# Coupling rows in column tiles and spread through DRAM, a room reserve that falls with attention's open buffers, and maxima added last in the score banks

## Chip, core and metric

The kernel runs on one core of one Trainium2 chip. The metric is device time in microseconds of that core, from the first to the last instruction and what lies around them; lower is better. The engines of the core are named as in the profile: PE (TensorE, matrix products; PEld is its weight load), DVE (VectorE), ACT (ScalarE), POOL (GpSimd) and SP (SyncE, which here issues every transfer).

## What is computed

Input `x` is 8 batches of 1024 tokens of 512 values, and `ctx` is 8 batches of 64 rows of 512 values; everything is float32.

- Attention: `x = x + Wo·attn(LN(x), ctx)` with 16 heads of 32 values. Queries and keys are rotated by one fixed phase per head, and each token attends to the 64 context rows of its batch.
- Feed-forward: with `out = LN(x)`, three cycles of `out = out + c·twist(out)` run. `twist` permutes and negates the four quarters of the 512 values. `c` is one number for each token and cycle: a network 512 → 512 → 256 → 128 → 1 with gelu after each hidden layer and a sigmoid at the end, times 0.3, plus a number per batch from a second small network of the mean over tokens, scaled by `adaptive_range`. At the end `x = x + out`.

## The kernel before, in words

**Work and its pieces.** The 8192 tokens are cut into 16 halves of 512 (`halves`, two for each batch). Attention runs over all halves first; then the feed-forward runs over "parts". `PARTS` cuts the first 14 halves into one part of 512 tokens each and the last two halves into two parts of 256 each, which makes 18 parts. `part_from_last[0]` counts them from 18 down to 1. Between the two phases `x` and the normalised `x` lie in DRAM (`x2d`, `xnd`).

**Numbers.** Most products are made of three matmuls in the type fp32r (`mm3`, lines 407 to 412): every operand is split into a high and a low half. A few products are plain float32 matmuls.

**Attention of a half** (`attn_half`, line 712). `qp` makes the queries, `sp` the approximate scores of which DVE takes the maximum per head, `mp` turns the maxima so that they lie along rows (`mT`), and the group of lines 772 to 785 builds four score banks `sT`: four matmuls of `hsel` with `mT` write minus the maximum into each whole bank (`start=True`), and then eight matmuls of `kT` with `qf` add the scores on 64 of the 128 partitions each. ACT takes the exponential into `pT`. `dn` sums the exponentials by 16 matmuls for each of two `k`, in column tiles: each writes only 32 of 128 partitions. The reciprocals go to DRAM (`rd`), and come back spread over partitions (`rb`, lines 810 to 820); `ap` and `op` make the output.

**Feed-forward of a part** (`ffn_part`, line 1017, W = 512 or 256 tokens). Stage A and B make the products `K`, `A` and `B`, which hold the first layer before any coupling: the input of cycle 1 is `A + c0·B`, and of cycle 2 it is `(1 - c0·c1)·A + (c0 + c1)·B`. `rest(cyc, h1)` (line 1048) makes the other layers: banks `l2`, `l3` (both `mm3`) and `l4`. In cycles 0 and 1, `l4` is one plain float32 matmul of `w4b` (the last layer's one column repeated 128 times) with `f3` over all W columns, so that the coupling row appears on all 128 partitions; in cycle 2 there are W/128 matmuls with `f3` as weights and one column. Line 1101 takes the tanh on ACT and line 1102 the scaling on DVE; the result `c` has 128 x W values in cycles 0 and 1. Lines 1121 to 1125 make `al = 1 - c0·c1` and `be = c0 + c1` over 128 x W. For the end of the part (`fin`) the first row of each goes to DRAM as `row` and comes back as `cc`, one value per token and partition (lines 1140 to 1146); POOL makes small factors from it, and ACT and DVE combine them with `x2` and `xt` into `out`. With `late`, an operation of cycle 2's start, the loads of `x2` and `xt` (2 MB for a part of 512) are held back.

**What orders the work.** Nothing is issued as it is written. `Plan` (line 119) notes every operation or group with its engine, its reads and writes and a cost in microseconds, and `schedule` (line 218) then walks an imagined clock: whenever an engine is free, it takes the ready operation with the lowest priority number whose buffers fit. A priority is the place in the text plus shifts by stage (`SHIFT`) and by part (`LAST`, and `TAIL` after time `FINALE`). Buffers live in `r4` (38 rooms of 4 KB per partition), `r2` (16 of 2 KB) and 8 PSUM banks; `CAPS` limits how many one kind may hold. The order so found is issued as it stands, so on the chip each engine keeps to it and waits where an operand is late.

**The reserve.** While any operation of attention is not done (`early_left`), an operation of the feed-forward may take a room of `r4` only if `KEEP` = 13 stay free (lines 205 to 206):

```
        for room, bs in need.items():
            keep = self.keep.get(room, 0) if op.late and self.early_left else 0
            if len(self.rooms[room]) < len(bs) + keep:
                return False
```

The functions the change touches, and what calls them:

Of the kernel before, what the change touches and what calls it, by code (L numbers as in the profile page):

```python
# [26 lines left out]
EPS = 1e-5  # L27
ROOMS4, ROOMS2 = 38, 16
GATE = 12
KEEP = 13  # L30
WIDE = 4
POOLED = 99
PLAIN = [(1, 1), (1, 2)]
CAPS = {'xb': 8, 'wn': 5, 'bv': 1, 'bo': 1, 'jm': 1, 'rt': 1, 'kbd': 2, 'vbd': 2, 'pT': 9, 'acc': 2, 'w3': 3, 'w2f': 1, 'w3f': 1, 'h2': 9, 'w4': 1, 'gw2': 1, 'gw3': 1, 'fxn': 2, 'fs': 2, 'f1': 12, 'AB': 14, 'f2': 11, 'f3': 2, 'c': 10, 'x2': 4, 'xe': 13, 'aT': 5, 'wg': 6, 'w2': 2, 'h1': 5, 'xna': 14, 'xnf': 6, 'xT': 6, 'fxT': 10, 'p': 6, 'sp': 4, 'pp': 2, 'ap': 4, 'op': 2, 'qp': 3, 'xp': 1, 'K': 4, 'A': 4, 'B': 7, 'l2': 5, 'l3': 4, 'l4': 5, 'ct': 3, 'qf': 5, 'qr': 3, 'rb': 4, 'mT': 2, 'mw': 1, 'sT': 8, 'mp': 3, 'dn': 1}
PARTS = [1, 1, 1, 1, 1, 1, 1, 1, 1, 1, 1, 1, 1, 1, 2, 2]
LAST = {4: -100, 2: -280, 1: -300}
FINALE = 1180
TAIL = {('fin', 4): 360, ('c1', 6): -57, ('load', 3): -330, ('A', 3): -389, ('B', 3): -170, ('c0', 3): -360, ('c1', 3): -130, ('c2', 3): 88, ('fin', 3): -160, ('fin', 6): -215, ('c0', 1): -350, ('fin', 5): 375, ('fin', 1): -170, ('c0', 4): 20, ('load', 6): 53, ('A', 6): 106, ('B', 6): 198, ('c0', 6): 157, ('c2', 6): 61, ('B', 4): 107, ('c0', 2): 110, ('c2', 4): 52, ('c2', 5): 416, ('load', 1): -320, ('A', 1): -24, ('B', 1): 73, ('c1', 1): -40, ('c2', 1): 33, ('A', 2): -40, ('load', 4): -117, ('A', 5): 50, ('load', 5): -136, ('B', 5): 150, ('c0', 5): 93, ('c1', 5): -264, ('fin', 2): 400, ('load', 2): 81, ('c2', 2): 30, ('B', 2): 120, ('c1', 4): 110}
SHIFT = {'ln1': 61, 'q': 175, 'm': 184, 's': -75, 'o': -41, 'pp': -40, 'av': 32, 'ln2': -260, 'load': -303, 'A': -70, 'B': -16, 'c0': -85, 'c1': 8, 'c2': 120, 'fin': -68}


def ts(i, n):
    return slice(i * n, (i + 1) * n)
# [3 lines left out]
    return t.bitcast(F32)  # L47

# [15 lines left out]
class Buf:  # L64


    def __init__(self, make, shape, room=None, tag=None, cap=0):
        self.make, self.shape, self.room, self.tag, self.cap = make, shape, room, tag, cap
        self.ap = None
        self.writers, self.readers = {}, {}  # L70
        self.left = 0
        self.slot = None


class View:
# [47 lines left out]
class Plan:  # L123


    def __init__(self, tc):
        self.tc, self.nc, self.ops, self.items = tc, tc.nc, [], None
        self.rooms, self.pools, self.caps = {}, {}, {}
        self.gates, self.stage = [], (None, 0)

        self.late, self.early_left, self.keep = False, 0, {}
# [35 lines left out]
    def add(self, cost, items, also):  # L167
        op = Op()
        op.engine, op.cost, op.calls, op.n = items[0][0], cost, [i[2] for i in items], len(self.ops)
        op.deps, op.users, bufs = set(self.gates), [], {}  # L170
        for _, _, _, reads, writes, _ in items:
            for v in reads:
                for k in v.grains():
                    if k in v.buf.writers:
                        op.deps.add(v.buf.writers[k])
                    v.buf.readers.setdefault(k, set()).add(op)
                bufs[id(v.buf)] = v.buf
            for v in writes:
# [8 lines left out]
        op.deps.discard(op)  # L187
        op.marks = [m for i in items for m in i[5] if isinstance(m, AF)]
# [24 lines left out]

    def schedule(self):
# [9 lines left out]
        now, seq = 0.0, itertools.count()  # L224
        while done < len(ops):
            for e in engines:
                if free[e] > now:
# [29 lines left out]
            while events and events[0][0] <= now + 1e-9:  # L257
# [1 line left out]
                if op is None:  # L259
                    continue  # L260
                done += 1
                self.early_left -= not op.late
                for b in op.bufs:
                    b.left -= 1
                    if b.left == 0:
# [19 lines left out]
class Engine:  # L285
# [3 lines left out]
    def __getattr__(self, method):  # L289
        def call(*args, **kw):  # L290
# [14 lines left out]
            def issue():  # L305
                f = getattr(getattr(self.plan.nc, self.name), method)
                f(*map(real, args), **{k: real(a) for k, a in kw.items()})  # L307

            self.plan.note(self.name, cost, issue, reads, outs, args)

        return call
# [37 lines left out]
def tile_xattn_ffn(  # L349
# [364 lines left out]
    def attn_half(b, h, xb, xnT):  # L714
# [53 lines left out]
        for k in range(2):  # L768
# [248 lines left out]
    def ffn_part(b, h, t0, n, xT):  # L1017
# [25 lines left out]
        for m in range(NC):  # L1043
            j, i = m // 2, m % 2
            p = product("B", m, 2)
            pl.vector.tensor_tensor(Bt[j][:, i, :], p, Bt[j][:, i, :], ALU.add)

        def rest(cyc, h1):
            nmc = f"{nm}_{cyc}"
            p = [bank([P, W], "l2", f"l2_{nmc}_{m}") for m in range(2)]  # L1050
# [33 lines left out]
                low(hL, f2[:, dc, :], hH)  # L1084
                mm3(p, w3p[0][:, dc, :], w3p[1][:, dc, :], hH, hL, dc == 0, dc == 1)
            gelu(f3, p, o3)
            if cyc < CYCLES - 1:
                p = bank([P, W], "l4", f"l4_{nmc}")
                c = t2([P, W], "c", f"c_{nmc}")
                pl.tensor.matmul(p, lhsT=w4b, rhs=f3, start=True, stop=True)  # L1090
            else:
# [3 lines left out]
                with pl.group(also=(c,)):  # L1095
                    for t in range(n):
# [4 lines left out]
            activation(c, p, AF.Tanh, bias=hb[:, 0:1], scale=0.5)  # L1101
            pl.vector.tensor_scalar(c, c, ar3, ca[:, b : b + 1], ALU.mult, ALU.add)
            return c

        def wide(t):
            return t.rearrange("p (o k) -> p o k", o=1).to_broadcast([P, 2, W])

        stage("c0")
        c0 = rest(0, h1)
        stage("c1")  # L1110
        h1, f1 = [], two(W, "f1", f"f1_{nm}_1_")
        for j in range(NC // 2):
# [5 lines left out]
            h1.append(f)  # L1118
        c1 = rest(1, h1)
        stage("c2")  # L1120
        al = t2([P, W], "c", f"al_{nm}")
        be = t2([P, W], "c", f"be_{nm}")
# [15 lines left out]
        stage("fin")  # L1138

        cc = small([P, 2, n], "cc", f"cc_{nm}", 2)  # L1140
        row = pl.fixed(dram.tile([1, 2, W], F32, name=f"row_{nm}"), [1, 2, W], F32)
        for k, t in enumerate((al, be)):
            with pl.group(cost=(0.1, 2.0)):
                pl.sync.dma_start(out=row[:, k, :], in_=t[:1, :])
# [19 lines left out]
        pl.gpsimd.tensor_scalar(rc[:, 4, :], pc[:, 3, :], -1.0, None, ALU.mult)  # L1164
        stage("c2")
        c2 = rest(2, h1)
        stage("fin")
        fa = small([P, 5, n], "fa", f"fa_{nm}", 2)
        wide_c = c2.rearrange("p (o t) -> p o t", o=1).to_broadcast([P, 5, n])
# [74 lines left out]
```

## Time and profile before

| | us |
|---|---|
| time, median of 3 runs (1316.57 to 1321.34) | 1318.05 |
| the profiled execution's own time | 1320.79 |
| span in its trace | 1319.0 |
| PE busy in the span | 1275.5 (97%) |
| DVE busy | 1110.2 (84%) |
| ACT busy | 859.7 (65%) |
| POOL busy | 346.6 (26%) |

The span runs from the first to the last instruction in the trace; the profiled execution's own time is 1.8 us longer. In the trace a line such as `L307 PE MATMUL l<-f,w4b 128*128 128x512` is an instruction of the line that issues everything (307), with its engine, the buffer it writes (without its number: `l` is `l2`, `l3` or `l4`), those it reads, the weights' shape (128*128: 128 rows by 128 columns; 128*32: a column tile) and its output's shape. A plain float32 matmul appears as two records, an fp32r one as one. The start of each record is measured; its length includes the way through the array, so the time a matmul takes from PE is read from the distance of starts.

### The profile page before, as it was taken

To read this page: it belongs to the slowest core of one execution; us is meant where nothing else is said; L and a number is where in the kernel's file an instruction comes from. 1 tells how busy PE (TensorE), PEld (TensorE's weight loads), DVE (VectorE), ACT (ScalarE), POOL (GpSimd) and SP (SyncE) were. 2 spreads that over 40 slices of the span, in tenths; PEclk is the share of its full clock that TensorE was granted. 3 is DMA by queue.
4 is the path that set the end of the run, shared out by engine and by line. 5 is a ranking of instruction groups with operands and counts; after the bars stand their busy time and mean duration, and the time that the engine had idled before them with its cause. 6 is when DMAs were issued, how large, how long until landed. Compare 5 with 4: busy or idle time off the path is not lost.

```text
span 1319.0 us, 21356 instructions
## 1 busy us (share of the span) xinstructions
PE 1275.5 (97%) x7907; PEld 994.9 (75%) x7907; DVE 1110.2 (84%) x1823; ACT 859.7 (65%) x1499; POOL 346.6 (26%) x426
## 2 busy tenths in 40 slices
PE   7999999999999999987999999999999999999996
PEld 6867776766767676755788888887888888888996
DVE  6767878787888787867869988899989999899997
ACT  3753545454553636433468878987889778888988
POOL 3501425152433424322201120112203121011271
PEclk9999999999999999998999999999999999999998
DMA  6313424243334444264302432324313233133224
GB/s 224 120 34 112 150 77 165 76 144 96 134 110 136 125 133 130 98 177 151 106 33 65 128 128 73 102 83 128 129 64 120 73 128 128 64 101 92 97 65 160
DMA packets 96152, 147.17 MB, mean 112 GB/s; under 512 B 25592, under 2 KB 47380, under 8 KB 96048
## 3 DMA queue, kind: packets, MB, share of 16 engines
q1 hardware_dynamic: 96048, 145.81, 34.6%
q8 instruction: 62, 1.02, 0.3%
q14 instruction: 42, 0.34, 0.1%
HBM read 93.80 MB, written 51.97 MB: 111 GB/s over the span
## 4 chain that ended last, share of the span: by engine, by line
PE 58%; DVE 6%; ACT 3%; issue 1%; DMA 1%; POOL 0%; SPq 0%; ACTq 0%; DVEq 0%
PE l L307 26%; PE op L307 6%; PE qp L307 3%; PE xp_f L307 2%; PE B_3p L307 2%; PE sT L307 2%; PE B_0p L307 2%; PE B_1p L307 2%; PE B_2p L307 2%; PE K_2p L307 2%; PE K_3p L307 2%; PE K_0p L307 2%; PE K_1p L307 2%; PE A_1p L307 1%; PE A_2p L307 1%; PE A_3p L307 1%
## 5 line engine op out<-in xcount | busy, mean ns | idle before, releaser
L307 PE MATMUL l<-h,w2H 128*128 128x512 f32 (+1 forms) x832 | 246.5, 381 | 0.1
L307 PEld LDWEIGHTS l<-h,w2H 128*128 128x128 f32 x832 | 149.6, 189 | 30.5 <-issue 3.6
L307 POOL TENSOR_TENSOR pc<-cc,rs 128x4 f32<-128x4 f32 (+1 forms) x18 | 22.2, 1231 | 507.3 <-DMA cc<-row 398.7
L307 PE MATMUL l<-h,w2L 128*128 128x512 f32 (+1 forms) x416 | 154.2, 371 | 0.0
L307 ACT ACTIVATE f<-l,bcol 128x512 f32<-128x512 f32 (+1 forms) x162 | 99.8, 635 | 28.5 <-PE l L307 26.9
L307 DVE TENSOR_TENSOR h<-f,h 128x1024 fp32r<-128x1024 f32 x84 | 102.1, 1218 | 12.9 <-ACT h L307 10.7
L307 ACT ACTIVATE f<-f,bcol 128x512 f32<-128x512 f32 x112 | 76.3, 721 | 46.0 <-DVE f L307 45.9
L307 POOL TENSOR_TENSOR acc<-acc,xnf 128x512 f32<-128x512 f32 x64 | 88.8, 1388 | 28.6 <-ACT xnf L307 25.2
L307 POOL TENSOR_TENSOR xb<-xb,bo_b 128x512 f32<-128x512 f32 x64 | 81.7, 1303 | 49.4 <-ACT xna L307 45.1
L307 DVE TENSOR_REDUCE mx<-sp 128x8 f32<-128x512 f32 x128 | 83.5, 680 | 9.9 <-PE sp L307 9.6
L307 ACT ACTIVATE pT<-sT 128x512 f32<-128x512 f32 x128 | 66.3, 612 | 36.7 <-PE sT L307 21.3
L307 PEld LDWEIGHTS l<-h,w2L 128*128 128x128 f32 x416 | 78.4, 188 | 13.7
L307 ACT CAST h<-f 128x1024 fp32r<-128x1024 f32 x84 | 88.0, 1053 | 0.7
L307 ACT CAST xT_a_0H<-xp_a 128x512 fp32r<-128x512 f32 x32 | 18.8, 587 | 97.7 <-PE xp_a L307 97.7
L307 ACT ACTIVATE xna<-xb,mb_a,rs_a 128x512 f32<-128x512 f32 x64 | 47.6, 829 | 51.2 <-DVE mb_a L307 38.9
L307 DVE TENSOR_TENSOR xb<-op,xb 128x512 f32<-128x512 f32 x64 | 44.2, 690 | 40.5 <-PE op L307 40.3
L307 POOL TENSOR_TENSOR rs<-rs,mhalf 128x4 f32<-128x4 f32 x16 | 19.4, 1215 | 205.7 <-DVE rs L307 205.1
L307 DVE TENSOR_SCALAR pT<-pT 128x1024 f32<-128x1024 f32 x64 | 44.5, 695 | 30.1 <-ACT pT L307 29.5
L307 DVE TENSOR_TENSOR f<-f,A 128x1024 f32<-128x1024 f32 x56 | 67.7, 1214 | 0.0
L307 ACT ACTIVATE x<-x,fa 128x256 f32<-128x256 f32 x128 | 65.3, 592 | 2.6 <-DVE fa L307 2.6
L307 ACT ACTIVATE xnf<-xb,mb,rs 128x512 f32<-128x512 f32 x64 | 47.4, 807 | 23.1 <-DVE mb L307 19.2
L307 DVE SCALAR_TENSOR_TENSOR x<-xt,fa,x 128x256 f32<-128x256 f32 x128 | 55.6, 480 | 6.2 <-ACT x L307 6.1
(399 smaller groups left out, 3737.3 us busy)
## 6 DMA issues: line engine op xcount, KB each, us to landing
xb<-in_x_dram SPq DMA_DIRECT2D x32, 512.0 KB
rb<-rd SPq DMA_DIRECT2D x128, 128.0 KB
x2d<-xb SPq DMA_DIRECT2D x32, 512.0 KB
xnd<-xnf SPq DMA_DIRECT2D x64, 256.0 KB
fxn<-xnd SPq DMA_DIRECT2D x32, 512.0 KB
x<-x2d SPq DMA_DIRECT2D x32, 512.0 KB
xt<-x2d SPq DMA_DIRECT2D x64, 256.0 KB
out_dram<-x SPq DMA_DIRECT2D x32, 512.0 KB
```

Source lines behind the costliest of these rows:

```text
L307: f(*map(real, args), **{k: real(a) for k, a in kw.items()})
```

## The change

- **Compact couplings.** Except for the last two parts (`DIRECT` = 2), `l4` becomes, in all three cycles, W/128 plain float32 matmuls with 32 columns of weights, each over 128 tokens and writing 32 partitions of one 128 x 128 bank. Tanh and scaling then run on 128 x 128 (64 x 128 in parts of 256), and so do `be` and `al`, whose last step moves from ACT to DVE. Each row is written to DRAM from one partition in 32 (`row_of`) and read back: `c0`, `be` and `al` over all 128 partitions x W (`spread`), and the cycle-2 row as one value per token and partition. `cc` is read by two transfers in place of one.
- **Reserve.** An operation of the feed-forward keeps free the smaller of 14 rooms and the number of attention's `r4` buffers that have not been given a room yet.
- **Scores.** The eight `kT` matmuls come first (`start=True` on 64 partitions each) and the four with the maxima last.
- **Planner.** It adds 0.18 or 0.1 us where PE changes to or from plain float32; caps are changed (among others `h2` 9 to 11, `f1` 12 to 14, `f2` 11 to 7, `c` 10 to 12, `x2` 4 to 6, `h1` 5 to 8, `xT` 6 to 9, `fxT` 10 to 12), and so are many shifts (`ln2` -260 to 165, `c2` 120 to 302, `c1` 8 to 115, `fin` -68 to 83) and the tail's entries; `FINALE` 1180 to 1160.

```diff
-KEEP = 13
+KEEP = 14
 WIDE = 4
+DIRECT = 2
...
+        op.keep = self.keep if self.late else {}
         op.late = self.late
-        self.early_left += not op.late
+        if not op.late:
+            for b in op.bufs:
+                if not b.counted:
+                    b.counted = True
+                    self.early_bufs[b.room] = self.early_bufs.get(b.room, 0) + 1
...
-            keep = self.keep.get(room, 0) if op.late and self.early_left else 0
+            keep = min(op.keep.get(room, 0), self.early_bufs.get(room, 0))
...
+                        if b.counted:
+                            self.early_bufs[b.room] -= 1
...
+                if e == "tensor" and not op.turn:
+
+                    busy += CHANGE[op.plain] if op.plain != plain else 0.0
+                    plain = op.plain
...
-                for g in range(4):
-                    q = slice(DK * g, DK * g + DK)
-                    pl.tensor.matmul(
-                        ps4[g], lhsT=hsel[q, ts(k, 2), :].rearrange("p r j -> p (r j)"),
-                        rhs=mT[q, :], start=True, stop=False,
-                    )
                 for r in range(2):
                     for g in range(4):
                         q = slice(DK * g, DK * g + DK)
                         pl.tensor.matmul(
                             ps4[g][ts(r, LC), :], lhsT=kT[q, 2 * k + r, ts(b, LC)],
-                            rhs=qf[k][q, r, :], start=False, stop=True,
+                            rhs=qf[k][q, r, :], start=True, stop=False,
                         )
+                for g in range(4):
+                    q = slice(DK * g, DK * g + DK)
+                    pl.tensor.matmul(
+                        ps4[g], lhsT=hsel[q, ts(k, 2), :].rearrange("p r j -> p (r j)"),
+                        rhs=mT[q, :], start=False, stop=True,
+                    )
...
+        compact = not 0 < part_from_last[0] <= DIRECT
...
-            if cyc < CYCLES - 1:
+            if compact:
+
+                p = bank([P, P], "l4", f"l4_{nmc}")
+                p = p[: DK * n, :]
+                c = small([P, P], "cs", f"c_{nmc}", 4)[: DK * n, :]
+                with pl.group(cost=0.27, also=(c,)):
+                    for t in range(n):
+                        pl.tensor.matmul(
+                            p[ts(t, DK), :], lhsT=w4b[:, :DK], rhs=f3[:, ts(t, P)],
+                            start=True, stop=True,
+                        )
+            elif cyc < CYCLES - 1:
...
+        def row_of(c, name):
+
+            r = pl.fixed(dram.tile([1, W], F32, name=f"{name}_{nm}"), [1, W], F32)
+            with pl.group(cost=(0.47, 2.0)):
+                if compact:
+                    pl.sync.dma_start(
+                        out=r.rearrange("o (t p) -> (o t) p", p=P), in_=c[0 : DK * n : DK, :]
+                    )
+                else:
+                    pl.sync.dma_start(out=r, in_=c[:1, :])
+            return r
+
+        def spread(r, name):
+            c = t2([P, W], "c", f"{name}_{nm}")
+            with pl.group(cost=(0.47, 2.5)):
+                pl.sync.dma_start(
+                    out=c,
+                    in_=r.via(lambda a: a.rearrange("o w -> (o w)").partition_broadcast(P)),
+                )
             return c
...
-        c0 = rest(0, h1)
+        c0 = c0s = rest(0, h1)
+        if compact:
+            c0 = spread(row_of(c0, "c0r"), "c0")
...
-        pl.vector.tensor_tensor(al, c0, c1, ALU.mult)
-        pl.scalar.activation(al, al, AF.Identity, bias=1.0, scale=-1.0)
-        pl.vector.tensor_tensor(be, c0, c1, ALU.add)
+        pl.vector.tensor_tensor(be, c0s, c1, ALU.add)
+        pl.vector.tensor_tensor(al, c0s, c1, ALU.mult)
+        pl.vector.tensor_scalar(al, al, -1.0, 1.0, ALU.mult, ALU.add)
+        be_r, al_r = row_of(be, "ber"), row_of(al, "alr")
+        if compact:
+            be, al = spread(be_r, "be"), spread(al_r, "al")
...
-        with pl.group(cost=(0.5, 4.0)):
-            pl.sync.dma_start(out=cc, in_=row.rearrange("o k (t p) -> p (o k) t", p=P))
+        for k, r in enumerate((al_r, be_r)):
+            with pl.group(cost=(0.5, 4.0)):
+                pl.sync.dma_start(out=cc[:, k, :], in_=r.rearrange("o (t p) -> p (o t)", p=P))
...
         c2 = rest(2, h1)
+        if compact:
+            c2_r, c2 = row_of(c2, "c2r"), small([P, n], "c2", f"c2_{nm}", 2)
+            with pl.group(cost=(0.5, 4.0)):
+                pl.sync.dma_start(out=c2, in_=c2_r.rearrange("o (t p) -> p (o t)", p=P))
```

More of the change, by code (lines that the diff above doesn't have):

```diff
@@ L29 @@
 GATE = 12
-KEEP = 13
+KEEP = 14
 WIDE = 4
+DIRECT = 2
 POOLED = 99
 PLAIN = [(1, 1), (1, 2)]
-CAPS = {'xb': 8, 'wn': 5, 'bv': 1, 'bo': 1, 'jm': 1, 'rt': 1, 'kbd': 2, 'vbd': 2, 'pT': 9, 'acc': 2, 'w3': 3, 'w2f': 1, 'w3f': 1, 'h2': 9, 'w4': 1, 'gw2': 1, 'gw3': 1, 'fxn': 2, 'fs': 2, 'f1': 12, 'AB': 14, 'f2': 11, 'f3': 2, 'c': 10, 'x2': 4, 'xe': 13, 'aT': 5, 'wg': 6, 'w2': 2, 'h1': 5, 'xna': 14, 'xnf': 6, 'xT': 6, 'fxT': 10, 'p': 6, 'sp': 4, 'pp': 2, 'ap': 4, 'op': 2, 'qp': 3, 'xp': 1, 'K': 4, 'A': 4, 'B': 7, 'l2': 5, 'l3': 4, 'l4': 5, 'ct': 3, 'qf': 5, 'qr': 3, 'rb': 4, 'mT': 2, 'mw': 1, 'sT': 8, 'mp': 3, 'dn': 1}
+CAPS = {'xb': 8, 'wn': 5, 'bv': 1, 'bo': 1, 'jm': 1, 'rt': 1, 'kbd': 2, 'vbd': 2, 'pT': 9, 'acc': 2, 'w3': 3, 'w2f': 1, 'w3f': 1, 'h2': 11, 'w4': 1, 'gw2': 1, 'gw3': 1, 'fxn': 2, 'fs': 4, 'f1': 14, 'AB': 14, 'f2': 7, 'f3': 4, 'c': 12, 'x2': 6, 'xe': 13, 'aT': 7, 'wg': 6, 'w2': 2, 'h1': 8, 'xna': 14, 'xnf': 8, 'xT': 9, 'fxT': 12, 'p': 6, 'sp': 4, 'pp': 2, 'ap': 4, 'op': 2, 'qp': 3, 'xp': 1, 'K': 4, 'A': 6, 'B': 5, 'l2': 6, 'l3': 6, 'l4': 3, 'ct': 3, 'qf': 4, 'qr': 5, 'rb': 4, 'mT': 2, 'mw': 1, 'sT': 8, 'mp': 4, 'dn': 1}
@@ L35 @@
 PARTS = [1, 1, 1, 1, 1, 1, 1, 1, 1, 1, 1, 1, 1, 1, 2, 2]
-LAST = {4: -100, 2: -280, 1: -300}
-FINALE = 1180
-TAIL = {('fin', 4): 360, ('c1', 6): -57, ('load', 3): -330, ('A', 3): -389, ('B', 3): -170, ('c0', 3): -360, ('c1', 3): -130, ('c2', 3): 88, ('fin', 3): -160, ('fin', 6): -215, ('c0', 1): -350, ('fin', 5): 375, ('fin', 1): -170, ('c0', 4): 20, ('load', 6): 53, ('A', 6): 106, ('B', 6): 198, ('c0', 6): 157, ('c2', 6): 61, ('B', 4): 107, ('c0', 2): 110, ('c2', 4): 52, ('c2', 5): 416, ('load', 1): -320, ('A', 1): -24, ('B', 1): 73, ('c1', 1): -40, ('c2', 1): 33, ('A', 2): -40, ('load', 4): -117, ('A', 5): 50, ('load', 5): -136, ('B', 5): 150, ('c0', 5): 93, ('c1', 5): -264, ('fin', 2): 400, ('load', 2): 81, ('c2', 2): 30, ('B', 2): 120, ('c1', 4): 110}
@@ L39 @@
-SHIFT = {'ln1': 61, 'q': 175, 'm': 184, 's': -75, 'o': -41, 'pp': -40, 'av': 32, 'ln2': -260, 'load': -303, 'A': -70, 'B': -16, 'c0': -85, 'c1': 8, 'c2': 120, 'fin': -68}
+LAST = {4: -100, 2: -280, 1: -280}
+FINALE = 1160
+TAIL = {('fin', 4): 360, ('c1', 6): -57, ('load', 3): -330, ('A', 3): -389, ('B', 3): -170, ('c0', 3): -372, ('c1', 3): -130, ('c2', 3): 92, ('fin', 3): -160, ('fin', 6): -215, ('c0', 1): -350, ('fin', 5): 375, ('fin', 1): -170, ('c0', 4): 20, ('load', 6): 53, ('A', 6): 10, ('B', 6): 93, ('c0', 6): 157, ('c2', 6): 61, ('B', 4): 107, ('c0', 2): 110, ('c2', 4): 52, ('c2', 5): 416, ('load', 1): -320, ('A', 1): -24, ('B', 1): 73, ('c1', 1): -40, ('c2', 1): 33, ('A', 2): -40, ('load', 4): -117, ('A', 5): 72, ('load', 5): -136, ('B', 5): 172, ('c0', 5): 88, ('c1', 5): -264, ('fin', 2): 434, ('load', 2): 81, ('c2', 2): 18, ('B', 2): 120, ('c1', 4): 94, ('c1', 2): 43}
@@ L42, in ts @@
+SHIFT = {'ln1': 61, 'q': 194, 'm': 184, 's': -112, 'o': -48, 'pp': -25, 'av': -16, 'ln2': 165, 'load': -302, 'A': -85, 'B': -59, 'c0': -93, 'c1': 115, 'c2': 302, 'fin': 83}
 def ts(i, n):
@@ L47, in f32 @@
     return t.bitcast(F32)
+CHANGE = (0.18, 0.1)
 GRAIN = 64
@@ L72, in __init__ @@
         self.slot = None
+        self.counted = False
 class View:
@@ L129, in __init__ @@
         self.gates, self.stage = [], (None, 0)
-        self.late, self.early_left, self.keep = False, 0, {}
+        self.late, self.early_bufs, self.keep = False, {}, {}
         for name in ("tensor", "vector", "scalar", "gpsimd", "sync"):
@@ L187, in add @@
         op.deps.discard(op)
+        op.plain = any(c.plain for c in op.calls) and op.engine == "tensor"
+        op.turn = all(c.turn for c in op.calls)
         op.marks = [m for i in items for m in i[5] if isinstance(m, AF)]
@@ L223, in schedule @@
         events, order, done = [], [], 0
-        now, seq = 0.0, itertools.count()
+        now, seq, plain = 0.0, itertools.count(), False
         while done < len(ops):
@@ L261, in schedule @@
                 done += 1
-                self.early_left -= not op.late
                 for b in op.bufs:
@@ L307, in issue @@
                 f(*map(real, args), **{k: real(a) for k, a in kw.items()})
+            issue.plain = method == "matmul" and kw["rhs"].dtype == F32
+            issue.turn = method == "transpose"
             self.plan.note(self.name, cost, issue, reads, outs, args)
@@ L1100, in rest @@
                         )
-            activation(c, p, AF.Tanh, bias=hb[:, 0:1], scale=0.5)
-            pl.vector.tensor_scalar(c, c, ar3, ca[:, b : b + 1], ALU.mult, ALU.add)
+            q = slice(0, DK * n if compact else P)
+            activation(c, p, AF.Tanh, bias=hb[q, 0:1], scale=0.5)
+            pl.vector.tensor_scalar(c, c, ar3[q, :], ca[q, b : b + 1], ALU.mult, ALU.add)
+            return c
+        def row_of(c, name):
[15 more added lines that the diff above has]
+                )
             return c
@@ L1120, in ffn_part @@
         stage("c2")
-        al = t2([P, W], "c", f"al_{nm}")
-        be = t2([P, W], "c", f"be_{nm}")
-        pl.vector.tensor_tensor(al, c0, c1, ALU.mult)
-        pl.scalar.activation(al, al, AF.Identity, bias=1.0, scale=-1.0)
-        pl.vector.tensor_tensor(be, c0, c1, ALU.add)
+        if compact:
+            al, be = (small([P, P], "abs", f"{k}s_{nm}", 4)[: DK * n, :] for k in ("al", "be"))
+        else:
+            al, be = (t2([P, W], "c", f"{k}_{nm}") for k in ("al", "be"))
+        pl.vector.tensor_tensor(be, c0s, c1, ALU.add)
[4 more added lines that the diff above has]
+            be, al = spread(be_r, "be"), spread(al_r, "al")
         h1, f1 = [], two(W, "f1", f"f1_{nm}_2_")
@@ L1140, in ffn_part @@
         cc = small([P, 2, n], "cc", f"cc_{nm}", 2)
[L1141 to L1144, printed above, removed]
-        with pl.group(cost=(0.5, 4.0)):
-            pl.sync.dma_start(out=cc, in_=row.rearrange("o k (t p) -> p (o k) t", p=P))
+        for k, r in enumerate((al_r, be_r)):
+            with pl.group(cost=(0.5, 4.0)):
+                pl.sync.dma_start(out=cc[:, k, :], in_=r.rearrange("o (t p) -> p (o t)", p=P))
         pc, rc = (small([P, 5, n], k, f"{k}_{nm}", 2) for k in ("pc", "rc"))
@@ L1166, in ffn_part @@
         c2 = rest(2, h1)
+        if compact:
+            c2_r, c2 = row_of(c2, "c2r"), small([P, n], "c2", f"c2_{nm}", 2)
+            with pl.group(cost=(0.5, 4.0)):
+                pl.sync.dma_start(out=c2, in_=c2_r.rearrange("o (t p) -> p (o t)", p=P))
         stage("fin")
```

## The prediction

> **What bounds the kernel now.** I read the busy table by stage first, then the chain of waits, then PE's instructions one by one around each operation that changes. The stage table, whose columns are stretch, length, then busy us and instructions of PE, PEld, DVE, ACT and POOL, granted clock, DMA share and GB/s:
>
> ```profile
> 660.00:1300.00 640.00, 639.94 (x3197) 531.37 (x3195) 583.90 (x873) 524.69 (x943) 121.17 (x192) 1.00 0.30 96
> ```
>
> From 660 to 1300, nearly the whole feed-forward, PE is never idle and its clock is full; DVE is at 91% and ACT at 82%. So a microsecond of PE work removed here is a microsecond of the end, as long as DVE (91%) doesn't become the pace. The chain of work that ended last says the same: it runs along PE, and one part of 512 tokens follows the last at an even pitch:
>
> ```profile
> 829.21 1.36 PE K_3p L307 x6
> ...
> 1119.22 1.37 PE K_3p L307 x6
> ```
>
> Seven parts in 290.01 us are 41.43 us a part. Of that DVE is busy 38.2 (92.2% in the same view's rows from 700 to 1100).
>
> The other place is the end of attention, where PE is neither busy nor at full clock. The same view, by tens:
>
> ```profile
> 580.00:590.00 10.00, 4.76 (x26) 3.41 (x24) 8.15 (x14) 3.73 (x7) 0.00 (x0) 0.90 0.92 232
> 590.00:600.00 10.00, 8.88 (x129) 3.24 (x136) 5.84 (x9) 5.35 (x11) 0.00 (x0) 0.76 0.19 39
> 600.00:610.00 10.00, 7.87 (x46) 5.65 (x31) 7.34 (x11) 2.09 (x2) 0.00 (x0) 1.00 0.35 82
> 610.00:620.00 10.00, 6.84 (x53) 4.00 (x52) 7.50 (x16) 2.49 (x4) 2.54 (x3) 0.94 0.64 215
> 620.00:630.00 10.00, 9.72 (x32) 7.78 (x33) 6.73 (x8) 2.32 (x3) 5.83 (x3) 0.72 0.73 233
> ```
>
> Length minus busy time times clock is 5.7, 3.3, 2.1, 3.6 and 3.0 us lost; with 1.2 at 570, 1.3 at 640 and 2.2 at 650, about 22 us from 570 to 660. The waits there: `mp` of the last half on DVE's `mw` (4.5 and 4.7), `op` on `aT_0H` (1.6), `K_0p` on `wg_0L` (3.4).
>
> **Compact couplings on PE.** What a float32 `l4` matmul costs now:
>
> ```profile
> 1115.87 0.39 PE L307 MATMUL K_1p<-fxT,wg_0L 128*128 128x512 f32 x1
> 1116.09 1.05 PE L307 MATMUL l<-f,w4b 128*128 128x512 f32 x2
> 1116.57 1.02 PE L307 MATMUL K_1p<-fxT,wg_0H 128*128 128x512 f32 x2
> 1117.43 0.40 PE L307 MATMUL K_1p<-fxT,wg_0L 128*128 128x512 f32 x1
> ```
>
> From its start to the third row behind it are 1.34 us, and an fp32r pair alone takes 0.455 (two steps of 0.228): 0.885. The same reading at 1147.72 and 1190.09 gives 0.855 and 0.865, so 0.87. The cycle-2 form (eight records at 1133.63; the matmul after the next pair starts at 1134.99) costs 0.90. The new form, four tiles of 32 columns over 128 tokens, is not run as `l4`, but `dn` has the very shape:
>
> ```profile
> 312.95 0.40 PE L307 MATMUL qp<-xT_a_0H,wq_0L 128*128 128x512 f32 x1
> ...
> 316.17 1.08 PE L307 MATMUL dn<-pT,dsel 128*32 128x128 f32 x32
> 317.18 0.50 PE L307 MATMUL qp<-xT_a_1H,wq_1H 128*128 128x512 f32 x1
> 317.51 0.40 PE L307 MATMUL qp<-xT_a_1L,wq_1H 128*128 128x512 f32 x1
> ```
>
> Sixteen take 1.01, so four take 0.25. At its edges to full-width fp32r the trace shows 0.10 more ahead of a group (312.95 + 0.23 is 313.18, the `dn` there starts at 313.28) and 0.10 behind (0.33 from 317.18 to 317.51 in place of 0.23). A lone group of four pays both edges: 0.45; without them 0.25 is the other end. I take 0.45, since every `l4` in the built order stands between fp32r groups. Saved: 28 matmuls of cycles 0 and 1 times 0.42 is 11.8; 14 of cycle 2 times 0.45 is 6.3; the two compact parts of 256 about 0.4, because a 256-column `l4` costs only about 0.52 (at 1220.62). Together **-18.5**, between that and -27 at 0.25.
>
> The Trainium skill, page TensorEngine Tiling (Array Packing), section Tiling Modes, speaks against a full gain: changing the tiling mode drains TensorE, while its overview promises up to four times with 32 columns. The two edges of 0.10 agree with the drain; by the promise alone the 0.87 would become 0.22 and the sum about -28.
>
> **DVE and ACT in a part.** Tanh on 128 columns instead of 512 saves ACT about 0.3 twice, and the `al` step (0.63) leaves it. On DVE the scaling (0.543 at 512) falls to about 0.3 twice; `al` and `be` (0.69 and 0.68) to about 0.29, by the line through 0.418 at 256 and 0.685 at 512; the moved step adds 0.2. DVE goes from 38.2 to 37.1 a part, PE from 41.4 to 40.1 (two times 0.42 and 0.45 less): the spare is 3.0. So the gain is not eaten by DVE, if no new wait enters its queue.
>
> **The new wait.** `c0` now goes to DRAM and back before DVE multiplies. The nearest rows are the old `row` and `cc`:
>
> ```profile
> 697.01 0.25 SPq L307 DMA_DIRECT2D row<-al  x1
> ...
> 698.20 0.39 SPq L307 DMA_DIRECT2D cc<-row  x1
> ...
> 700.51 0.92 POOL L307 TENSOR_TENSOR pc<-cc,rs 128x4 f32<-128x4 f32 x1 [50.50 <-DMA cc<-row]
> ```
>
> The read is issued 1.19 after the write and used 2.31 later: 3.5 us. The spread moves 256 KB, which at the 264 GB/s of the fullest slice needs 1.0 more: 4.5 is the other end. I take 4.0. Behind a waiting `f<-B,c` stands all of DVE's queue, so cover is what the built order puts on DVE between the scaling of `c0` and that multiply: 3.9, 3.8, 6.2, 3.0, 8.4, 3.6, 2.9, 2.6, 11.7, 2.9, 2.6, 8.4, 6.2 and 8.2 us for the 14 parts, from durations of these rows. Short by 7 us in sum at 4.0, 11 at 4.5, none at 2.6. DVE's spare is 14 times 3.0 or 42, and PE has 18 to 40 us of other matmuls between `l4` and the next `l2` (11 to 20 before), so most is hidden: **+3**, between 0 and 11. `be` and `al` have 4.7 and more, the cycle-2 row 5.5 and more, and are costed at nothing; without that cover each would cost up to 4 a part. The 114 added transfers take SP about 0.3 each, 34 us of a queue that mostly waits; POOL's `cc` has tens of us of slack.
>
> The skill's page DMA: Bandwidth & Descriptors, section Anatomy of one DMA, gives about 2 us fixed per DMA (fitted on the GpSimd path), most of it the write receipt. Two and 0.6 of data would be 4.6 us, about 12 short in sum, and the total 1 us higher; the trace's 3.5 for two smaller ones is below that.
>
> **The end of attention.** The reserve now falls with attention's open buffers. In the built order `dn_7_1` and `ap_7_1`, between which lies the trip of `rd` and `rb`, have 84 matmuls of stages K, A, B and `l2` between them (19 us), and `mp_7_1` stands behind the 48 of `op_6_1`. Of PE's work before the last attention matmul 24 us are feed-forward, 4 before. The four last `sp` groups still stand directly ahead of `mp_7_1`, so some 4 us stay; `K_0p` stands at the same distance in PE work as before (520 us), so its 3.4 stays, as do 2 at `gs` and `gT`, with 3 of slow clock: 12 of 22. Gain **-10**, between -22 (all) and +5 (if the tighter order only moves the wait to `wg_0L`).
>
> **Scores.** The same twelve matmuls in another order; the inner change of type stays, the outer one moves from ahead to behind. PE waited 1.2 for `mT` ahead of `hsel`, now covered by the `kT` matmuls: **-1**, within 3.2 either way (32 groups, one edge of 0.10).
>
> **The tail.** `c2` of `7_0_2` is compact, and four matmuls from the last in PE's order; it pays a trip of about 4 us where the before finished both last parts together. ACT and DVE do the other's `x` meanwhile: **+2**, between -2 (DVE is at 98% from 1200 to 1300 and loses work) and +6.
>
> **Sum.** -18.5 + 3 - 10 - 1 + 2 is -24.5. From the span of 1319.0 that is 1294.5; the profiled execution took 1320.79 and would take 1296.3; the median of the runs lies 2.7 below that execution, so **1293.5**.
>
> **Rivals.**
> - More: groups at 0.25 (-27) and a hole filled by 18: about 1277. For it: the 0.27 that the plan itself charges; against it: both edges are measured.
> - Less: the hole stays, since its waits are DVE's and DMA's and more PE work behind them doesn't shorten them. -18.5 + 3 - 1 + 2 is -14.5, 1303.5. If DVE also sets the pace (it is at 100% from 1250 to 1280), its 1.1 a part, 15 in all, takes the place of the 18.5: 1307.
> - About no change: the hole stays, the wait costs its 11 and the tail its 6: -2.5, 1315.5.
> - Slower: spreads of `c0` wait behind bulk loads. SP's built order puts the 2 MB of `x2` and `xt`, or `fxn` and `out`, directly ahead of `c0r` in about 8 parts of 14; 2 MB at 264 GB/s take 7.9 us. It happens already: the last `rd` is issued at 577.59 behind a 512 KB `fxn`, and the first `rb` can only follow at 582.66, five us later, against 1.2 at 601.81. DVE would wait 7.9 + 4.0 less a cover of 3, 8.9 us; 3.0 of it is spare, and 5.9 in 8 parts are 47: 1341. It decides from waits of 6.1 us in eight parts (3.0, and 24.5 / 8). Against it: the loads wait for their own buffers and for `late`, so few of the eight coincide, and PE has its 18 us of other matmuls.
>
> **Chances.** Forecast (1284 to 1302) 0.50; more 0.13; less (1302 to 1311) 0.18; no change 0.09; slower 0.10. A measurement here tells about 0.5%, 6.6 us, from no change: faster 0.81, within 0.09, slower 0.10. The range 1272 to 1314 leaves out the slower case, most of the no-change case (0.07) and the far end of "more" (0.03): 0.20.
>
> **What would show it.** Right: `l<-f,w4b` with 128*32 weights and a start-to-start cost of 0.45; the pitch of `K_3p` near 40.1; about 12 us lost from 570 to 660; DVE's waits for DMA on `c` below 15 us in sum. Wrong: a pitch of 41 or more with DVE idle on `c<-c0r` (slower rival), or DVE above 97% with PE idle on `h` (less).

## The result and the profile after

| | before | after |
|---|---|---|
| time, median (4 runs each, alternating) | 1319.53 us (1316.57 to 1321.34) | 1303.93 us (1302.71 to 1306.16) |
| ratio, 95% interval | | 0.9886 (0.9861 to 0.9911) |
| the profiled execution's own time, its span | 1320.79, 1319.0 us | 1303.96, 1302.2 us |

The forecast was 1293.5: the change gained 15.6 us where 24.5 were forecast. The measured time lies 2 us above the forecast's band (1284 to 1302), in the band that the prediction gave to the rival "less". To see where the gain came from, I summed what PE loses in each stretch as the prediction did (length minus busy time times clock, here in steps of 5 us), in the one profiled execution of each kernel; what is left of the span is PE's work.

| us | before | after | difference | forecast |
|---|---|---|---|---|
| PE's work | 1266.3 | 1254.4 | -11.9 | -18.5 |
| lost, 0 to 560 | 20.0 | 17.4 | -2.6 | -1 (scores) |
| lost, 560 to 660 | 22.4 | 11.2 | -11.2 | -10 |
| lost, 660 to 1200 | 0.0 | 1.8 | +1.8 | +3 |
| lost, from 1200 | 10.3 | 17.4 | +7.1 | +2 |
| span | 1319.0 | 1302.2 | -16.8 | -24.5 |

Two terms are off, each by about 5 to 7 us: PE's work and the tail. The table is good to about 2 us: in the executions profiled below, the first 60 us alone lost between 9.1 and 11.5. And waits that are shorter than the overlap of two matmul records count as work: experiments 2 and 6 add no PE instruction, and their row "PE's work" is 7.0 and 4.6 higher. The stage table of the kernel after, with the columns as before:

```profile
570.00:580.00 10.00, 4.79 (x25) 3.93 (x24) 7.73 (x17) 1.57 (x3) 1.70 (x2) 0.84 0.97 269
...
600.00:610.00 10.00, 10.00 (x102) 8.09 (x101) 10.00 (x22) 2.90 (x5) 1.44 (x1) 1.00 0.57 189
```

```profile
580.93 1.11 PE L322 MATMUL mp<-ident,mw 128*128 128x128 f32 x4 [6.13 <-DVE mw L322]
```

```profile
660.00:1300.00 640.00, 623.54 (x3346) 504.74 (x3345) 575.86 (x917) 518.51 (x947) 84.87 (x216) 0.99 0.38 118
700.00:1100.00 400.00, 398.50 (x1971) 314.26 (x1970) 357.36 (x517) 317.62 (x533) 47.42 (x120) 1.00 0.40 121
1200.00:1300.00 100.00, 85.33 (x599) 75.71 (x597) 91.34 (x194) 85.27 (x193) 22.58 (x60) 0.95 0.44 142
```

The hole at the end of attention is now mainly one wait, of 6.13 us, between 574 and 581, and the lower clock behind it; from 600 to 610, where the before lost 2.1, PE is busy throughout. From 700 to 1100 PE idles 1.5 us in 400. In the last stretch PE is busy 85.33 of 100 and DVE still 91.34. The same row of the kernel before:

```profile
1200.00:1300.00 100.00, 99.94 (x712) 93.56 (x710) 97.50 (x192) 88.80 (x206) 37.56 (x47) 1.00 0.29 94
```

The two rows don't cover the same work: PE's last matmul ends at 1291.8 after and at 1310.5 before, so 8.2 us of the 14.7 that PE is not busy here lie behind its last matmul. From that matmul to the end of the span are 10.4 us, before 8.5. The rest of the tail's loss are PE's waits, 6.2 us in all where the before had 1.5, and each of the long ones is for a gelu output of ACT:

```profile
1283.41 1.13 PE L322 MATMUL l<-f__14137,w2f 128*128 128x256 f32 x4 [1.07 <-ACT f__14137 L322]
...
1290.80 1.01 PE L322 MATMUL l<-bcol,f 128*128 128x1 f32 x4 [3.59 <-ACT f L322]
```

The gelu of the second wait could not start before 1290.28, because eight output steps of an earlier part stood ahead of it in ACT's queue:

```profile
1286.35 4.03 ACT L322 ACTIVATE x<-x,fa 128x256 f32<-128x256 f32 x8
```

The new waits on the spread couplings, DVE's view of waits from 660 to 1300 (us in total, times, longest):

```profile
DVE f L322 <- DMA c<-c0r: 3.0, 4, 1.1
...
DVE A L322 <- DMA al<-alr: 2.1, 1, 2.1
DVE f L322 <- DMA be<-ber: 1.6, 2, 1.4
```

So DVE waits for `c0r` in 4 of the 14 parts of 512. And this is what a compact group costs (`x8` are its four matmuls, two records each):

```profile
924.73 0.39 PE L322 MATMUL l<-h,w2L 128*128 128x512 f32 x1
925.04 0.42 PE L322 MATMUL l<-f,w4b 128*32 128x128 f32 x8
925.40 0.73 PE L322 MATMUL l<-h,w2H 128*128 128x512 f32 x2
925.97 0.40 PE L322 MATMUL l<-h,w2L 128*128 128x512 f32 x1
```

The product at 924.73 would be done at 924.96 (0.23); the third product behind the group starts at 925.97, and the two before it (`x2`) take 0.455. That leaves 925.97 - 924.96 - 0.455 = 0.555 for the group. The rows around 931.75 and 940.50 give the same. The prediction had 0.45.

### The profile page after: what moved, and what is told of

It is laid out like the page before. It is cut to its first block, busy times and chain, and to the rows that moved or that the text cites. A ratio compares the mean times of both kernels' runs of the same rounds, so it can differ in the third digit from the quotient of the medians.

```text
span 1302.2 us, 21969 instructions
## 1 busy us (share of the span) xinstructions
PE 1258.0 (97%) x8083; PEld 967.4 (74%) x8083; DVE 1094.8 (84%) x1841; ACT 846.1 (65%) x1481; POOL 313.6 (24%) x426
## 4 chain that ended last, share of the span: by engine, by line
PE 76%; DVE 11%; ACT 7%; issue 2%; POOL 2%; DMA 2%; SPq 0%; ACTq 0%; DVEq 0%; POOLq 0%
PE l L322 21%; PE op L322 13%; PE qp L322 10%; PE sT L322 3%; PE ap L322 2%; PE sp L322 2%; PE xp_f L322 2%; PE xp_a L322 2%; PE A_2p L322 2%; PE K_3p L322 2%; ACT x L322 2%; PE K_2p L322 2%; PE K_0p L322 1%; PE K_1p L322 1%; PE A_1p L322 1%
## 5 line engine op out<-in xcount | busy, mean ns | idle before, releaser
L322 POOL TENSOR_TENSOR pc<-cc,rs 128x4 f32<-128x4 f32 (+1 forms) x18 | 11.5, 640 | 537.4 <-DMA cc<-ber 445.4
L322 POOL TENSOR_TENSOR xb<-xb,bo_b 128x512 f32<-128x512 f32 x64 | 91.9, 1463 | 44.7 <-ACT xna L322 42.6
L322 ACT ACTIVATE f<-f,bcol 128x512 f32<-128x512 f32 x112 | 77.4, 724 | 16.8 <-DVE f L322 16.6
L322 ACT ACTIVATE qf<-qp,bqr 128x512 f32<-128x512 f32 x64 | 43.9, 692 | 24.5 <-PE qp L322 24.0
```

## The experiments

Each ran beside the kernel before. "Against the changed kernel" is the difference of the two ratios to before, times 1319.5; the intervals of two ratios together make it uncertain by about 4 us.

**1. The price of a group.** Every compact `l4` group issues its products twice, everything else in the order of the changed kernel.

```diff
-                    for t in range(n):
+                    for t in [*range(n), *range(n)]:
```

> The changed kernel, with every compact l4 group's matmuls issued twice (the second set overwrites the first with the same values). Nothing else moves: the order on every engine is that of the changed kernel. In its trace a lone group of four costs PE 0.555 us (start of the row after the next fp32r pair less the pair's own 0.455), where the prediction had 0.45. Theory, fixed part: four tiles stream in about 0.22 and the rest is paid once by a group, 0.34 for entering, leaving and emptying; then a second set adds 0.22 to each of 42 groups of four and 0.11 to each of six groups of two, 9.9 us, all of it in the time where PE sets the pace: 1312 to 1315. Rival A, every set of four costs 0.36 by itself: 15 to 17 more, 1319 to 1321. Rival B, PE is no longer the pace of the feed-forward (DVE is): less than 4 more, under 1308.

1315.12 us, ratio 0.9975 (0.9954 to 0.9995): 11.7 more than the changed kernel; PE's work rose by 9.9, to 1264.3. In PE's rows:

```profile
931.82 0.64 PE L322 MATMUL l<-f,w4b 128*32 128x128 f32 x16
932.40 0.74 PE L322 MATMUL l<-h,w2H 128*128 128x512 f32 x2
```

From the group to the next row are 0.58 us in place of 0.36, so four more products cost 0.22. Of the 0.555 of a lone group 0.335 are then fixed, paid once. The theory held: 9.9 us more of PE work were expected and found, and all of it arrives at the end, within what can be told.

**2. A longer trip.** `c0`'s row is copied once more in DRAM before it is spread (16 more transfers), the order kept.

```diff
+                if name == "c0":
+                    r2 = pl.fixed(dram.tile([1, W], F32, name=f"{name}hop_{nm}"), [1, W], F32)
+                    pl.sync.dma_start(out=r2, in_=r)
+                    r = r2
```

> The changed kernel, with one more copy in the way of c0: the row goes from DRAM to a second row in DRAM before it is spread, so each of 16 trips is longer by a transfer and its completion (1.2 to 2.3 us by the rows of the old trip). The order on DVE, ACT, PE and POOL is that of the changed kernel. Theory: the trip lies beside other DVE work and PE's 18 us and more of other matmuls; DVE waited 3.0 us for c0r in all, will wait some 15 to 25 more, and the time grows by 2 to 7 us. Rival, the trip is on the path that sets the end: 14 to 16 times 2 us, 28 or more, over 1330.

1318.1 us, ratio 0.999 (0.9975 to 1.0005): 13.7 more. Both theories missed. DVE's waits and then PE's, from 660 on:

```profile
DVE f L322 <- DMA c<-c0hop: 21.0, 12, 3.3
```

```profile
PE l L322 <- DVE h L322: 3.8, 6, 1.2
PE l L322 <- DVE h_0L L322: 2.0, 4, 1.0
```

DVE waited 18 to 20 us longer, as expected, but about 0.7 of it came through (0.5 to 1, with the uncertainty): PE's `l` products wait for the `h` that DVE makes behind the late multiply. A spare that the busy times show is not one that the fixed order can use.

**3. Scores as before**, the rest as changed.

> The changed kernel with the maxima first in the score banks again, as in the kernel before; only the order inside 32 PE groups differs. Theory: the twelve matmuls cost the same either way and the wait for mT was 1.2 us before: 0 to 2 us slower. Rival: the new order is worth an edge of 0.1 or more per group at both ends, or hides mT by more: 3 to 8 us slower.

1305.94 us, ratio 0.9896 (0.9874 to 0.9918): 1.3 more, not to be told from nothing. From 60 to 560 us PE loses 8.3 here as in the changed kernel, against 10.5 before, so the 2.2 saved there don't come from the scores.

**4. The cycle-2 trip in the tail.** In the parts 5, 4 and 3 from the last, `l4` of cycle 2 takes the old form, without the trip through DRAM; the order of the tail changes with it.

```diff
-            if compact:
+            if compact and not (cyc == CYCLES - 1 and 0 < part_from_last[0] <= 5):
...
```

> The changed kernel with the cycle-2 row of parts 5, 4 and 3 from the last in the old form (four or two matmuls with f3 as weights, no trip through DRAM); the order differs only in the last part of the work. In the trace of the changed kernel the cycle-2 row of part 5 (6_1_0) is written at 1277.3 and its use starts at 1285.6, 8.3 us later, with x2 and xt loads of 1 MB between the two transfers, and eight ACT steps of that part then stand ahead of the last gelu, for which PE waits 3.6 us. Theory, trips in the tail cost: 3 to 6 us faster, about 1299. Rival, ACT's and DVE's work for the last four parts sets the end whichever way the row comes: within 1.5 us of the changed kernel.

1311.17 us, ratio 0.9932 (0.9906 to 0.9958): 6.1 more. Both missed. PE waits once, at 1282 to 1288, for a gelu that comes late behind the queues of DVE and ACT; from 1280 to 1290 DVE is busy 9.93 of 10 us:

```profile
PE l L322 <- ACT f__14137 L322: 6.2, 1, 6.2
```

As the order of the tail changed too, the run doesn't price the trip by itself; it shows that leaving it out gains nothing in the order then found. The changed kernel's own trace has no wait of any engine for `c2r`, so the trip is not what its tail pays. What paces it then may be DVE; the next run asks.

**5. More DVE work in the tail.** In the last four parts the multiply `f<-B,be` is issued twice: 5.4 us of DVE, order kept.

> The changed kernel with every order kept; in the last four parts of 256 tokens the multiply of B with be is issued twice (same result), 8 more DVE instructions of about 0.68 us, 5.4 us of DVE work and no PE work. Theory after the run that put the old cycle-2 row back: from about 1200 us on DVE, not PE, sets the pace, so nearly all of it shows at the end: +4 to +6 over the changed kernel, 1308 to 1310. Rival: PE and the trips set the end there and DVE has room: under +1.5, 1304 to 1305.5.

1311.0 us, ratio 0.9941 (0.9921 to 0.9961): 7.3 more, above the 4 to 6 of the theory and far from the rival. In the trace PE's loss from 1200 on grows from 17.4 to 21.3; another 2.9 of the longer span are lost before 560, where nothing was changed. So 3.9 us or more of the 5.4 arrive, and whether all of it does can't be told. The stage table of this kernel:

```profile
1250.00:1260.00 10.00, 8.85 (x58) 7.47 (x56) 9.85 (x21) 5.01 (x13) 0.00 (x0) 1.00 0.24 81
1260.00:1270.00 10.00, 9.07 (x52) 7.72 (x51) 9.93 (x20) 8.58 (x21) 5.63 (x12) 1.00 0.35 102
1270.00:1280.00 10.00, 8.57 (x58) 6.47 (x56) 9.89 (x19) 7.77 (x19) 0.00 (x0) 1.00 0.56 188
```

DVE is full, PE is not: here, from 1230 to 1290, DVE (98 to 100% of each 10 us) sets the pace. In the changed kernel DVE is at 92 to 100% of each 10 us from 1230 to 1280, and at 70% from 1280 to 1300, where the order on ACT holds PE up.

**6. More DVE work in the steady parts.** In the 14 parts of 512 the first multiply of `B` with `c0` is issued twice: 17 us of DVE, order kept.

> The changed kernel with every order kept; in the 14 parts of 512 tokens the first multiply of B with c0 is issued twice (same result), one more DVE instruction of about 1.2 us a part, 17 us in all, and no PE work. Theory of the prediction, that DVE has 3 us to spare in each part: under +3, up to 1307. Theory after the run with the extra hop, where 20 us more of DVE waiting cost 13.7: DVE's room is used up by the fixed order, PE waits for what comes late behind the multiply: +8 to +13, 1312 to 1317. In the steady stretch PE's idle time from 700 to 1100 tells it apart: 1.5 us now, 6 or more by the second.

1316.99 us, ratio 0.999 (0.9975 to 1.0005): 13.7 more. PE idles 6.7 us from 700 to 1100 in place of 1.5, and its waits from 660 to 1300 are again for `h`:

```profile
PE l L322 <- DVE h L322: 3.0, 5, 1.0
PE l L322 <- DVE h_0L L322: 2.8, 5, 0.8
```

The second theory held (13.7 where it had 8 to 13). The prediction's 3.0 us of DVE's spare in a part is refuted: 1.2 us more a part cost about 1.0 (0.7 to 1.3, with the uncertainty).

**7. The reserve alone**, in the kernel before (`KEEP` 14 and the count of open buffers).

> The kernel before with the falling reserve alone (KEEP 14 and the count of attention's open buffers); couplings, scores, caps and shifts as before. Theory: the reserve is what fills the hole at the end of attention, 22.4 us lost there become about 11: 8 to 11 us faster than before, 1308 to 1311, and the tail as before. Rival: the shifts and caps that came with it (ln2, wg and the part of the last K) fill the hole, and the reserve alone is worth under 3: 1315 to 1319.

1322.24 us, ratio 1.0029 (1.0013 to 1.0046): slower than before. From 560 to 660 PE loses 18.5 us in place of 22.4; PE's waits there (before: 4.5 for `mw`, 3.4 for `wg_0L`) move to others more than they shrink:

```profile
PE op L314 <- DVE aT_1L L314: 3.2, 1, 3.2
...
PE mp L314 <- DVE mw L314: 1.8, 1, 1.8
```

The tail loses 13.4 in place of 10.3. The theory missed, and the rival's range too: the reserve by itself takes 3.9 us off the hole, not 11.2, and gains no time.

**8. The couplings alone undone** (`compact = False`, all else as changed; attention in the changed kernel's order).

> The changed kernel with the couplings as before (full-width l4 matmuls, no spread through DRAM, tanh and scaling on 128 x W), everything of attention in the changed kernel's order. Theory: the couplings save 13.6 us of PE work and cost about 3 to 5 of waits and tail, so this takes 1312 to 1316, losing only the gain at the end of attention (11) less some of the tail's loss. Rival: the couplings bring nothing, since DVE and the order set the pace: 1302 to 1306. The shifts were not set for this form, so a result above 1318 would tell of them and not of the couplings.

1324.57 us, ratio 1.0048 (1.0031 to 1.0065). It is above 1318, so by the expectation it tells of shifts set for the other form, and not of what the couplings are worth. One thing it does tell: from 560 to 660 PE loses 9.8, so the filled hole doesn't come from the couplings.

**9. The rest of the hole.** 20 operations are moved in the found order: `sp_7_1`'s last groups between the products of `op_6_1`, their maxima and `mw` behind them, `ap_7_0` ahead of `mp_7_1`, all transfers of `rb_7_0` together, the casts of `wg` behind `aT_7_0`.

```diff
+MOVES = [(2773, 2776), (2777, 2773), ...]
...
         order = self.schedule()
+        for a, b in MOVES:
+            op, ref = (next(o for o in order if o.n == k) for k in (a, b))
+            order.remove(op)
+            order.insert(order.index(ref) + 1, op)
```

> The changed kernel with 20 operations moved within the found order, all at the end of attention: the four last score groups of half 7_1 between the output matmuls of half 6_1, their maxima on DVE and mw directly behind them, the value products of half 7_0 ahead of mp, the four last transfers of rb directly behind the first four, and the casts of wg on DVE behind aT. Nothing of the feed-forward moves. Theory: what is left of the hole is a matter of order: PE's wait of 6.1 for mw and the half clock behind it (2 to 4) go, 11.2 lost from 560 to 660 become 3 to 5, and as everything behind is paced by PE and DVE together the end follows: 1296 to 1299. Rival: something else is late at the same time (the transfers of rb and of the weights wg), the wait moves to K or ap, and the gain is under 2: 1302 to 1306.

1303.83 us, ratio 0.9878 (0.9859 to 0.9896): nothing gained that can be told. `mp` ran at 576.74 in place of 580.93, but then:

```profile
582.03 2.00 PE L327 MATMUL sT<-qf,kT 32*64 32x512 f32 x10 [3.62 <-ACT mT L327]
```

`mT` stood behind four `xnf` on ACT. From 560 to 660 PE loses 8.9 in place of 11.2, but the first 60 us of this execution happened to lose 2.3 more, and the first `K_0p` came at 603.8 in place of 605.1. The rival's number held, but not its cause: the wait moved, not to `K` or `ap` behind transfers, but to the next operation that stood late in a queue.

**10. The reserve alone undone** (13 rooms until attention ends; all else as changed).

> The changed kernel with the reserve as before (13 rooms until the last operation of attention is done, in place of the smaller of 14 and the open buffers); couplings, scores, caps and shifts as changed. Theory after the run with the reserve alone, which left 18.5 us lost at the end of attention and came out slower: reserve, caps and shifts work only together, so the changed shifts without the falling reserve lose at least the 11 us of the hole: 1314 or more. Rival: the shifts alone fill the hole: 1302 to 1307.

1341.7 us, ratio 1.016 (1.0145 to 1.0175): 36 more than the changed kernel. From 560 to 660 PE loses 26.9 in place of 11.2, most of it in one wait:

```profile
PE op L325 <- ACT aT_0H L325: 17.2, 1, 17.2
```

That is the trip of `rd` and `rb` and what DVE and ACT do behind it, with no feed-forward work of PE beside it (the first `K_0p` comes at 639.9), as the reserve keeps the rooms. These 15.7 us are less than half of the 36: 8.2 more are lost from 660 to 1200 and 5.7 more from 1200 on, in an order that was set for the other reserve. With experiment 7: reserve, caps and shifts fill the hole together, and neither side does it alone.

**11. DVE relieved by POOL.** The multiplies of `A` with `al` move to POOL in all parts but the last four (34 us of DVE), caps and shifts set anew.

```diff
-POOLED = 99
+POOLED = 4
...
```

> The changed kernel with the two multiplies of A with al moved from DVE to POOL in all parts but the last four (28 instructions of 1.22 us, 34 us of DVE's work), and with caps and shifts set anew for it. POOL is 24% busy and takes 1.4 us for a product of 128 x 512, so about 2.8 for 128 x 1024. Theory: DVE's load is what PE's lateness in the steady stretch and the tail comes from (17 us more of it cost 13), so 34 us less give back the 1.5 of idle PE there and some of the 17 lost from 1200 on: 1293 to 1300. Rival: POOL and DVE slow each other down when both multiply (DVE's products of 128 x 1024 then show over 1.4 us in place of 1.22), and the result comes later: 1304 to 1320.

1362.11 us, ratio 1.0309 (1.0291 to 1.0328): 56 more than the changed kernel. POOL's two products, and DVE beside them:

```profile
828.54 5.52 POOL L322 TENSOR_TENSOR A<-A,al 128x1024 f32<-128x1024 f32 x2 [24.15 <-PE A_3p L322]
```

```profile
829.41 0.69 DVE L322 TENSOR_TENSOR A<-A_3p,B 128x512 f32<-128x512 f32 x1
830.08 1.76 DVE L322 TENSOR_SCALAR c<-c,ar,ca 128x128 f32<-128x128 f32 x1
831.76 3.38 DVE L322 TENSOR_TENSOR h<-f,h 128x1024 fp32r<-128x1024 f32 x1
```

While POOL multiplies (to 834.06), `c` takes 1.76 in place of 0.34, and `h` ends 1.08 behind POOL's end and takes 3.38 in place of 1.22; `A`, which has one operand in PSUM, takes its usual 0.69. So DVE isn't relieved, it is held: behind 660 us, 28 DVE instructions, as many as POOL's products, are longer than those of their shape in the changed kernel, by 50 us in sum, where 34 us were taken off. The rival had the mechanism, and its range was too small. These 16 us of DVE don't make 56, though: what the later `A` (POOL's two products take 5.5 us, DVE's 2.4) and the new order add was not told apart. The Trainium skill, page SBUF — State Buffer, section Who interferes with whom, has the rule: DVE and GpSimd share a port pair as an exclusive lock, and a DVE instruction with two inputs in SBUF contends with a GpSimd instruction that reads SBUF. The rows of `h` (two such inputs, 3.38 us) and of `A` (one, 0.69 us) agree; `c`, which has one tensor as input, is longer too, and that is not covered by the rule as given here.

**12. Both ends at once.** Experiment 9 with three more moves (`mp` and `mT` ahead of the `xnf`), and plain float32 `l2` and `l3` in cycle 2 of the parts 2 and 3, which takes splits off DVE, with the last parts' shifts set anew.

```diff
-PLAIN = [(1, 1), (1, 2)]
+PLAIN = [(1, 1), (1, 2), (2, 2), (3, 2)]
...
```

> The changed kernel with both places at which PE still loses time treated by order and by DVE's work. End of attention: the 20 moves of the run before, and three more, mp and ACT's mT ahead of the four xnf of half 6_1, and the first w1c behind the casts of wg, since PE then waited 3.6 for mT. Tail: cycle 2 of the parts 2 and 3 takes plain float32 products for l2 and l3, as cycles 1 and 2 of the last part do, which takes about 1.9 us each of splits from DVE and adds about 0.8 to PE, with the shifts of the last parts set anew. Theory: PE loses 4 to 6 us from 560 to 700 in place of 11.5, and the tail, paced by DVE, loses 12 to 15 from 1200 on in place of 17.4; if both carry to the end 1293 to 1298. Rival: the first half carries nothing, as the moves alone moved their wait and no time, because the weights' and rb's transfers (DMA at full share from 575 to 585) set when the feed-forward begins: then only the tail counts, 1299 to 1304, with PE reaching the first K no earlier than at 605.0.

1303.23 us, ratio 0.9885 (0.9865 to 0.9905): the same as the changed kernel. The wait moved once more, now to a sum of POOL behind the `xnf`:

```profile
586.64 1.02 PE L327 MATMUL gs<-acc,sel 128*8 128x512 f32 x2 [3.04 <-POOL acc L327]
```

From 560 to 700 PE loses 7.7 (theory 4 to 6), from 1200 on 14.5 (theory 12 to 15), but PE's work rose by 4.6, of which the expectation had 1.6. `K_0p` starts at 604.1, 1.0 earlier, although the first 60 us lost 1.0 more. Neither theory is cleanly met, and none of the twelve runs is faster than the changed kernel by more than the uncertainty.

## Why the prediction was right or wrong, by its steps

- **Compact couplings on PE, -18.5.** The direction held, the size didn't. The step that failed is "sixteen take 1.01, so four take 0.25": it spread over sixteen what a group pays once. Experiment 1 gives 0.22 for four products and 0.335 fixed, 0.555 and not 0.45. With it 28 times 0.315 and 14 times 0.345 are 13.6, and PE's work fell by 11.9; the 1.7 between them may be short waits that count as work, which no run shows. The two edges of 0.10 that I read at `dn` were part of the fixed share only: its 1.01 and the two edges, less four times 0.22, leave 0.33, so that row agrees with the new price.
- **DVE and ACT, a spare of 3.0 a part.** This step fell (experiments 2 and 6). The range of the new wait held, but for a smaller wait, not by the spare: DVE waited 3.0 us for `c0r` in all, where 7 were expected at 4.0 a trip. The waits for `be` and `al`, costed at nothing, were 1.6 and 2.8. At the rate of experiment 2 (0.7) these 7.4 us would cost about 5 (an estimate; taking them away wasn't tried), though PE's loss from 660 to 1200 is only 1.8.
- **The end of attention, -10.** Right in size (-11.2). Of what was said to stay, `mp`'s wait did (6.1 in place of "some 4"), `K_0p`'s 3.4 for `wg_0L` didn't; these two errors, 2 and 3 us in opposite directions, nearly cancel, so the size is in part luck. The cause was named too narrowly: not the falling reserve but reserve, caps and shifts together (7 and 10), and not the couplings (8).
- **Scores, -1.** Not shown: undoing them cost 1.3 with an uncertainty of 4, and changed nothing where PE's loss fell (experiment 3).
- **The tail, +2.** Too small by 5. I priced the trip of `c2`, and no engine waits for that trip. From 1230 to 1280 DVE is at 92 to 100% and its work counts (5), which fits that what PE saves in the last parts turns into its own idle time; the two longest waits, 3.6 and 1.1, are for gelus behind output steps in ACT's queue. How the 7.1 divide between DVE's load and that order is not shown. Nor is the share of the spreads in the tail: the chain of work that ended last passes there through the transfers of `be` (3.35) and `al` (4.33), costed at nothing, but DVE idles only 0.7 for them.
- **Rival "less".** Its 1303.5 is the measured time by luck: it needs the hole to stay, and the hole was halved. Its other half, DVE setting the pace, is what the tail shows, but it put that over the whole feed-forward.
- **Sum: "2.7 below that execution".** The profiled execution after the change lies at the median of its runs (1303.96 and 1303.93), not 2.7 below. So the span missed its forecast of 1294.5 by 7.7, and 2.7 of the 10.4 us by which the time missed are this term, which only described where one execution lay among three runs.
- **Slower by spreads behind bulk loads.** Not seen: the longest wait for `c0r` is 1.1 us, against the 8.9 that it needed.
- **What would show it.** Of the signs of being right, the hole (10.8 lost from 570 to 660, for 12) and DVE's waits on `c` (3.0, below 15) came; the group's cost (0.555, for 0.45) didn't. The pitch of `K_3p` can't be read after the change: the parts no longer follow evenly (747.61, 815.43 and 890.78, 910.49 are starts of neighbours in the chain of waits).

What stays open: what the compact couplings are worth in time by themselves, and how much of that is due to DVE's lighter load and how much to PE's; experiment 8 was to split them, and its order stood in the way.

## What to carry to other kernels

Price a small group by a lone one, or by two sizes: dividing a long run by its count hides what each group pays once. In an order that is fixed beforehand, a spare read from busy shares may hide little: delay the engine by a known amount and see how much arrives; here about 0.7 to 0.8 of it did where DVE was at 90% load, and at least as large a share (3.9 of 5.4) where it was full. A wait removed counts only up to the next one in the same queue, and settings that were chosen together can't be judged one by one.

## What the runs showed of the hardware

- A column-tiled float32 group between full-width fp32r products costs 0.335 us once and 0.22 for each four of its tiles (128 x 128 each).
- After waits of 3.6 and 6.1 us PE came back at a lower granted clock. The changed kernel waits 6.1; the run with the 20 moves, 3.6, and its clock over the next 10 us is about as low (0.67 and 0.65, against 0.50 and 0.80):

```profile
580.00:585.00 5.00, 4.07 (x36) 1.38 (x36) 2.71 (x3) 1.96 (x3) 4.53 (x4) 0.50 0.98 369
585.00:590.00 5.00, 5.00 (x50) 1.06 (x42) 5.00 (x8) 3.23 (x5) 0.00 (x0) 0.80 0.79 246
```

```profile
580.00:585.00 5.00, 2.97 (x22) 0.93 (x30) 2.44 (x3) 3.13 (x6) 4.54 (x4) 0.67 1.00 355
585.00:590.00 5.00, 5.00 (x28) 1.35 (x15) 4.96 (x8) 3.77 (x7) 0.00 (x0) 0.65 0.62 199
```

  The first fence is the changed kernel, the second the run with the moves; the eighth column is the clock.
- Beside POOL products over 128 x 1024 a DVE product with both inputs in SBUF took 3.38 us in place of 1.22, and one with an input in PSUM its usual 0.69 (experiment 11).
